# Expert results taken between the last expert blocks, in a four-layer kernel with two mixtures of experts in a row

## The chip, the cores and the metric

The kernel runs on one core of a Trainium2 chip. The metric is the device time of one execution in microseconds (us), smaller being better. Beside the run times there is one profiled execution of each kernel, from which all durations below come.

## The reference

`x` is (4, 512, 256) in float32: four batches of 512 tokens of 256 features. `ctx` is (4, 64, 256). Four layers follow one another, each with an attention onto the context and a feed-forward part, both added to `x`:

```python
# layer 0
x = x + cross_attention(layernorm(x), ctx)             # 16 heads
x = x + experts(layernorm(x), top2 of 8, F=704)        # SwiGLU experts
# layer 1
x = x + feature_map_attention(layernorm(x), ctx)       # exp(z), exp(-z) features
x = x + latent_attention(rmsnorm(x))                   # causal, 16 heads, rotary
x = x + shared_expert(n) + experts(n, top2 of 7, F=256)
# layer 2
s = unit(layernorm(x)) @ unit(ctx).T                   # (512, 64) a batch
x = x + ctx[argmax(s)]                                 # hard alignment
x = x + down(fp4(silu(fp4(n) @ Wg) * (fp4(n) @ Wu)))   # F=704, weights fp4 too
# layer 3
x = x + linear_attention(layernorm(x), ctx)
x = x + experts(layernorm(x), top2 of 8, F=512)
```

`experts` is, for each token, the sum of two expert outputs with the router's weights. `fp4` rounds groups of 16 values to a four-bit grid with a common scale.

## The kernel before

The 2048 tokens are 16 row tiles of 128 (`NT = 16`); a batch `g` is four of them (`GT = 4`). `x` stays on the chip for all four layers.

A mixture of experts is an object of class `Routed`. `route` scatters every token's normed row twice to DRAM (`xs`), in the order of its two experts. The sorted rows make 39 blocks of 128 rows (38 in layer 1), each with one expert. `blocks` loops over them. One pass of the loop over `b` has these parts:

- `up(b)`: transpose the 128 tokens (`ps_xe`, copied to `e_xT`), multiply by the gate and up weights (`ps_gu`), take silu on ACT (`e_s`) and the product on DVE (`e_h`). In its middle it calls `between`, which transposes the block before (`turn`: `ps_he`, `e_hT`) and takes a step of `routing`.
- `down(b-1)`: multiply by the down weights (`ps_de`), scale (`e_y`), and write the rows to `ys` in DRAM by an indirect DMA of POOL, the "put".
- a step of `other`, a generator of work for later; in layer 0 it quantises the weights of layer 2 (`l2_weights`: `w2y`, `ps_wq`, `w2q`).
- `weights(b+3)` and `tokens(b+5)` issue the loads of a later block on SP's queue: 1408 + 768 KB of weights in layer 0, 512 + 256 in layer 1, 1024 + 512 in layer 3, and 130 KB of tokens. `e_wgu` has three buffers, `e_wd` four and `e_x` five.

The rest of `other` is drained after the last `down`.

In the blocks, DVE's and SP's instructions stand in the order of the program text (`in_order`). Those of PE, ACT and POOL are ordered by a scheduler when the kernel is built, from estimated costs; in parts of the attentions PE's order is that of the text as well.

When the blocks are over, `load(t)` reads tile `t`'s two result rows per token from `ys` (256 KB, `e_r`) and `take(t)` adds them to `x[t]` in two adds of 128 x 256. Layer 1's `xattn` does that in `ctx_heads`, batch by batch, ahead of a layer norm (`ln_st`, `ln_mv`, `ln_sd`, `xn`), the transposes (`ps_xT`, `xnT`), the queries (`ps_qf`, `q`) and the first scores (`ps_cs`). Layer 2's `l2` loads its weights (2.1 MB) and prepares the context (`l2_context`: `csq`, `cnr`, `cn`, `ps_cn`), loads and takes all tiles, and then, for each batch, runs `l2_xattn` (norm, `ps_xT`, `sq`, `ps_sim`, the argmax `am_...`, `ps_oh`, `ps_al`), `normed` (a norm into `l2xn`) and, for each tile, `quantized` (`fp4` on DVE and POOL into `xq`, `ps_xq`) ahead of the products `ps_f`. At the end of layer 3 all 16 tiles are loaded, taken and stored to `out_x`, on two queues in turn.

The token order is such that `cuts` splits the blocks by batch: a block below `cuts[g+1]` needs tokens of batches 0 to `g` alone.

Of the kernel before, what the change touches and what calls it, by code (L numbers as in the profile page):

```python
# [22 lines left out]
P = 128  # L23
# [165 lines left out]
class Net:  # L189
# [427 lines left out]

    def ctx_heads(self, pool, st, query, values, bias, before):

        g = st.g  # L620
        if before:
            for i in range(GT):
                before.take(g * GT + i, self.nc.gpsimd if g else self.nc.vector)
        xn = self.xn_tile()
        self.layernorm(g, xn)
        for i in range(GT):
            x = self.x[g * GT + i]
            self.nc.gpsimd.tensor_tensor(x, x, self.row(bias), ALU.add)
        yield
        xT = self.transposed(xn)  # L630
        yield
        st.qs = query(pool, xT)
        yield
        st.va = values(pool, g)
        yield

    def xattn(self, query, values, scale, dv, W, bias, before=None, after=None, keys=None, begin=lambda: None):
# [4 lines left out]
        with self.room("xattn") as pool, self.banks(mm=4, sc=1), ExitStack() as stack:  # L642
# [9 lines left out]
            sts = [SimpleNamespace(g=g, pr=[]) for g in range(B)]  # L652

# [145 lines left out]
class Routed:  # L799
# [9 lines left out]
    def __init__(self, net, n, F, gu, d, name, stamp, w=None):  # L809
# [5 lines left out]
        self.scattered, self.put, self.loaded = [], [], {}  # L815
# [277 lines left out]
    def blocks(self, pool, routing, per=1, other=()):  # L1093
# [4 lines left out]
        other = iter(other)  # L1098
# [4 lines left out]
        def between():  # L1103
            nonlocal turned
            turned = last and self.turn(last[1])
            next(routing, None)

        for b in range(self.nb):
            now = self.up(b, between)
            if last:  # L1110
                self.down(turned, *last)
            last = now
            for _ in range(per - 1):
                next(routing, None)
            next(other, None)
            if b + 5 == self.cuts[-2]:
                for _ in routing:
                    pass
            self.weights(b + 3)
            self.tokens(b + 5)  # L1120
        between()
        self.down(turned, *last)
        for _ in other:
            pass

    def load(self, pool, t, eng, bufs=16):

        net = self.net
        rows = net.ys[self.stamp : self.stamp + 2 * NT * P].rearrange("(k t p) e -> t p k e", p=P, k=2)
        self.loaded[t] = pool.tile([P, 2, E], F32, tag="e_r", name="e_r", bufs=bufs)  # L1130
        eng.dma_start(self.loaded[t], rows[t])

    def take(self, t, eng):

        x, r = self.net.x[t], self.loaded.pop(t)
        for k in range(2):
            eng.tensor_tensor(x, x, r[:, k], ALU.add)


class Layers(Net):  # L1140
# [275 lines left out]
    def l1_ffn(self):  # L1416
        nc, d = self.nc, self.d
        moe = Routed(self, 7, E, d["e1gu"], d["e1d"], "e1", STAMP, w=V_LN2)
        with ExitStack() as stack:

            tail = self.tail = stack.enter_context(self.room("mla_tail"))
            mla, once = (stack.enter_context(ExitStack()) for _ in range(2))
# [18 lines left out]
            def soon():  # L1441
                once.close()
                moe.begin(stack.enter_context(self.room("l1h", side="right")))
# [4 lines left out]
            with self.room("l1b", side="right") as pool, self.banks(mm=4, tr=2, acc=2), self.in_order(DVE, SP):  # L1448
                moe.blocks(pool, last, 3)
        return moe  # L1450

    def l2_context(self, pool):
# [7 lines left out]
        nc.scalar.activation(nr, ss, AF.Sqrt)  # L1460
        nm = pool.tile([SC, B], F32, tag="cnm", name="cnm", bufs=1)
# [3 lines left out]
        cnT = pool.tile([P, NC, B, SC], F32, tag="cnT", name="cnT", bufs=1)  # L1465
        cn = pool.tile([SC, B, E], F32, tag="cn", name="cn", bufs=1)
        nc.vector.tensor_tensor(cn, self.ctx, rs[:, :, None].to_broadcast([SC, B, E]), ALU.mult)
        for c in range(NC):
# [4 lines left out]
        return cnT  # L1473

    def l2_xattn(self, pool, g, cnT):
# [3 lines left out]
        self.layernorm(g, xn)  # L1479
# [3 lines left out]
        nc.scalar.activation(l2, sq, AF.Sqrt)  # L1483
        nc.vector.tensor_scalar(lm, l2, 1e-12, None, ALU.max)
        nc.vector.reciprocal(lr, lm)
        ps = self.acc.tile([P, GT, SC], F32, tag="acc", name="ps_sim")
        for i in range(GT):
            for c in range(NC):
                nc.tensor.matmul(
                    ps[:, i], xT[:, c, i * P : (i + 1) * P], cnT[:, c, g], start=(c == 0), stop=(c == NC - 1)  # L1490
                )
        sim = pool.tile([P, GT, SC], F32, tag="sim", name="sim")
        nc.vector.tensor_tensor(sim, ps, lr[:, :, None].to_broadcast([P, GT, SC]), ALU.mult)
        _, oh = self.first_max(sim, SC, "am")
        pt = self.tr.tile([SC, GT, P], F32, tag="tr", name="ps_oh")
# [3 lines left out]
        nc.scalar.copy(ohT, pt)  # L1499
        for k in range(GT // 2):  # L1500
            pa = self.acc.tile([P, 2, E], F32, tag="acc", name="ps_al")
            for i in range(2):
                nc.tensor.matmul(pa[:, i], ohT[:, 2 * k + i], self.ctx[:, g], start=True, stop=True)
            for i in range(2):
                x = self.x[g * GT + 2 * k + i]
                nc.vector.tensor_tensor(x, pa[:, i], x, ALU.add)
# [92 lines left out]
    def l2(self, moe):  # L1599
        nc = self.nc  # L1600
        F, H = 704, 352
        with self.room("l2") as pool:
            wq = pool.tile([P, W2_END], F32, tag="w2", name="w2", bufs=1)
            whole = W2_END - E
            nc.sync.dma_start(wq[:, :whole], self.w2q[:, :whole])
            nc.sync.dma_start(wq[: F - 5 * P, whole:], self.w2q[: F - 5 * P, whole:])
            wg, wu = (wq[:, a : a + NC * F].rearrange("p (c f) -> p c f", c=NC) for a in (W2_GATE, W2_UP))
            wd = wq[:, W2_DOWN:].rearrange("p (f e) -> p f e", e=E)
            cnT = self.l2_context(pool)
            xns = {}  # L1610

            def tmp(tag, n):
                return pool.tile([P, n], F32, tag=f"{tag}{n}", name=tag)

            def quantized(t):

                g, i = divmod(t, GT)
                xq = pool.tile([P, E], F32, tag="xq", name="xq")
                self.fp4(tmp, xq, xns[g][:, i], nc.gpsimd)
                ps = self.tr.tile([P, NC, P], F32, tag="tr", name="ps_xq")  # L1620
                for c in range(NC):
                    nc.tensor.transpose(ps[:, c], xq[:, c * P : (c + 1) * P], self.ident)
                xT = pool.tile([P, NC, P], F32, tag="xqT", name="xqT")
                nc.scalar.copy(xT, ps)  # L1624
                return xT

            def up(xT):
                pss = []
                for k in range(2):
                    for w in (wg, wu):  # L1630
                        ps = self.mm.tile([P, 512], F32, tag="mm", name="ps_f")
                        for c in range(NC):
                            nc.tensor.matmul(  # L1633
                                ps[:, :H], xT[:, c], w[:, c, k * H : (k + 1) * H], start=(c == 0), stop=(c == NC - 1)
                            )
                        pss.append(ps)
                return pss

            def gated(pss):
                h = pool.tile([P, F], F32, tag="h", name="h")  # L1640
                for k in range(2):
                    s = pool.tile([P, H], F32, tag="fs", name="fs")
                    nc.scalar.activation(s, pss[2 * k][:, :H], AF.Silu)
                    nc.vector.tensor_tensor(h[:, k * H : (k + 1) * H], s, pss[2 * k + 1][:, :H], ALU.mult)
                hq = pool.tile([P, F], F32, tag="hq", name="hq")
                self.fp4(tmp, hq, h, nc.gpsimd)
                return hq

            def down(t, hq):
                hT = pool.tile([P, 6, P], F32, tag="hqT", name="hqT")  # L1650
                self.rows_to_columns(hq, lambda f0, n, r: hT[:r, f0 : f0 + n])
                po = self.acc.tile([P, 512], F32, tag="acc", name="ps_fd")
                for f in range(6):
                    r = min(P, F - f * P)
                    nc.tensor.matmul(po[:, :E], hT[:r, f], wd[:r, f], start=(f == 0), stop=(f == 5))
                nc.vector.tensor_tensor(self.x[t], po[:, :E], self.x[t], ALU.add)

            def normed(g):
                xns[g] = pool.tile([P, GT, E], F32, tag="l2xn", name="l2xn")
                self.layernorm(g, xns[g])  # L1660

            for t in range(NT):
                moe.load(pool, t, nc.scalar if t // GT == 1 else nc.sync)
            for t in range(2 * GT):
                moe.take(t, nc.vector if t < GT else nc.gpsimd)
            self.l2_xattn(pool, 0, cnT)
            normed(0)
            xT, last = quantized(0), None  # L1670
            for t in range(NT):
                g, i = divmod(t, GT)
                if g + 1 < B:
                    if i == 0:
                        if g + 2 < B:
                            for k in range(GT):
                                moe.take((g + 2) * GT + k, nc.gpsimd)
                        self.l2_xattn(pool, g + 1, cnT)
                    elif i == 2:
                        normed(g + 1)  # L1680
                pss = up(xT)
                if t + 1 < NT:
                    xT = quantized(t + 1)
                hq = gated(pss)
                if t:
                    down(t - 1, last)
                last = hq
            down(NT - 1, last)
# [45 lines left out]

# [45 lines left out]
```

## Time and profile before

| what | us |
|---|---|
| runs | 1991.52, 1987.32, 1986.11 (median 1987.32) |
| profiled execution | 1997.21 |
| its span | 1995.5 |
| PE busy in the span | 1712.2 |
| DVE busy in the span | 1020.4 |
| ACT busy, POOL busy | 671.4, 424.3 |
| expert blocks of layer 0 | about 165 to 530 |
| expert blocks of layer 1 | about 1180 to 1344 |
| expert blocks of layer 3 | about 1720 to 1966 |

Times in the profile count from the span's start. "Busy" is the time in which an engine executes an instruction. The granted clock (PEclk) is the share of full speed at which TensorE was let run; its mean over the span is 0.93. A row of the timeline gives start, duration, engine, line and operation, output and inputs, and in brackets the idle time of the engine before it with what ended that. Lines such as SPq and ACTq are DMA issues of the SP and ACT queues. A row of a window gives, for a stretch of time, the busy time of each engine, the granted clock, the busy share of the DMA engines and what they moved.

### The profile page before, as it was taken

How to read it: one execution, taken by the hardware profiler on the slowest of the kernel's cores; microseconds unless marked ns; L12 is line 12 of the kernel's file. 1: busy time of each engine (PE TensorE's matmuls, PEld its weight loads, DVE VectorE, ACT ScalarE, POOL GpSimd, SP SyncE). 2: the span in 40 equal slices, each digit the busy share in tenths (PEclk: the TensorE clock that was granted, in tenths of full speed). 3: DMA queues.
4: the chain of work that ended last, by engine and by line, in shares of the span. 5: the costliest groups of instructions: out<-in, count | busy, mean ns of one | idle time of the engine just before them, and what ended most of it. 6: DMA issues, size and time to landing. Idle time of an engine off the chain costs nothing.

```text
span 1995.5 us, 25928 instructions
## 1 busy us (share of the span) xinstructions
PE 1712.2 (86%) x8752; PEld 970.5 (49%) x8752; DVE 1020.4 (51%) x3011; ACT 671.4 (34%) x1254; POOL 424.3 (21%) x594
## 2 busy tenths in 40 slices
PE   5878999999789868898989888985998887899993
PEld 2435666666444433343433344543665443455552
DVE  3655544444454343444454536546989565553333
ACT  3333222222254323335343432233445334222220
POOL 2031211111240021123131312223113103221112
PEclk8989999999899968998999999995899898999997
DMA  9528787887400100000001035972000001788884
GB/s 294 160 84 330 273 294 281 290 287 281 134 1 1 39 1 1 1 1 22 1 27 42 19 101 173 298 254 85 1 1 1 12 1 65 238 293 301 298 298 162
DMA packets 109350, 271.61 MB, mean 136 GB/s; under 512 B 13409, under 2 KB 71201, under 8 KB 99105
## 3 DMA queue, kind: packets, MB, share of 16 engines
q1 hardware_dynamic: 82976, 227.97, 33.9%
q0 software_dynamic: 10176, 28.00, 3.7%
q10 hardware_dynamic: 16064, 13.98, 2.1%
q8 instruction: 70, 1.15, 0.2%
q14 instruction: 64, 0.52, 0.1%
HBM read 220.48 MB, written 49.42 MB: 135 GB/s over the span
## 4 chain that ended last, share of the span: by engine, by line
PE 69%; DVE 18%; ACT 6%; issue 3%; DMA 2%; POOL 1%; SPq 0%; ACTq 0%; DVEq 0%; POOLq 0%
PE ps_gu L1030 20%; PE ps_de L1072 10%; PE ps_ms L1235 4%; PE ps_mo L1273 3%; DVE mq L1240 2%; PE ps_p L612 2%; PE ps_mx L1250 2%; PE ps_f L1633 2%; PE ps_xT L377 2%; PE ps_he L1059 2%; PE ps_bc L591 2%; ACT cpr L563 2%; PE ps_cx L557 1%; PE ps_ms L1238 1%; PE ps_cy L597 1%
## 5 line engine op out<-in xcount | busy, mean ns | idle before, releaser
L1030 PE MATMUL ps_gu<-e_wgu,e_xT 128*128 128x352 f32 (+1 forms) x1088 | 420.9, 526 | 13.1 <-DVE e_xT L1022 5.8
L1030 PEld LDWEIGHTS ps_gu<-e_wgu,e_xT 128*128 128x128 f32 x1088 | 195.5, 190 | 155.7 <-issue 71.4
L1072 PE MATMUL ps_de<-e_wd,e_hT 128*128 128x256 f32 x932 | 233.0, 387 | 10.8 <-ACT e_hT L303 3.1
L1075 POOL DMA_INDIRECT ys<-e_y,e_to x116 | 113.2, 976 | 482.6 <-ACT e_y L1074 336.5
L1072 PEld LDWEIGHTS ps_de<-e_wd,e_hT 128*128 128x128 f32 x932 | 172.8, 191 | 83.6 <-issue 39.0
L1047 DVE TENSOR_TENSOR e_h<-e_s,ps_gu 128x352 f32<-128x352 f32 (+2 forms) x155 | 83.4, 538 | 244.8 <-PE ps_gu L1030 185.0
L1240 DVE TENSOR_REDUCE mq<-ps_ms 128x2 f32<-128x256 f32 (+3 forms) x128 | 105.7, 826 | 139.9 <-PE ps_ms L1238 136.6
L1046 ACT ACTIVATE e_s<-ps_gu 128x352 f32<-128x352 f32 (+2 forms) x155 | 74.1, 478 | 280.3 <-PE ps_gu L1030 264.9
L1074 ACT ACTIVATE e_y<-ps_de,e_wt 128x256 f32<-128x256 f32 x116 | 55.0, 474 | 262.6 <-PE ps_de L1072 250.0
L1252 ACT ACTIVATE mpr<-ps_mx 128x1024 f32<-128x1024 f32 (+3 forms) x128 | 90.1, 704 | 146.9 <-PE ps_mx L1250 137.9
L1235 PE MATMUL ps_ms<-mkT,mqT 32*128 32x512 f32 (+3 forms) x512 | 111.7, 515 | 25.8 <-DVE mq L1240 24.3
L859 POOL DMA_INDIRECT xs<-xn,e_at x96 | 94.5, 985 | 120.4 <-DVE e_fi L893 39.7
L1250 PE MATMUL ps_mx<-mqm,mkT 32*128 32x128 f32 (+3 forms) x512 | 107.4, 497 | 1.3 <-ACT mpr L1252 1.3
L1254 POOL TENSOR_SCALAR_AFFINE_SELECT mpr<-mpr 128x256 f32<-128x256 f32 x128 | 52.2, 409 | 250.7 <-ACT mpr L1252 250.6
L1273 PE MATMUL ps_mo<-mpr,va 128*32 128x128 f32 (+3 forms) x512 | 97.1, 461 | 4.5 <-POOL mpr L1254 3.2
L1633 PE MATMUL ps_f<-w,xqT 128*128 128x352 f32 x256 | 86.1, 478 | 1.2 <-ACT xqT L1624 1.2
L1059 PE MATMUL ps_he<-consts_sb,e_h 128*128 128x128 f32 x466 | 76.3, 277 | 9.6 <-DVE e_h L1047 6.7
L557 PE MATMUL ps_cx<-q,kbd 32*128 32x512 f32 x256 | 45.2, 806 | 44.1 <-ACT cpr L563 44.1
L1235 PEld LDWEIGHTS ps_ms<-mkT,mqT 32*128 32x128 f32 x512 | 40.9, 195 | 80.6 <-DVE mq L1240 56.0
L1019 DVE COPY e_xT<-ps_xe 128x256 f32<-128x256 f32 x78 | 33.0, 423 | 86.7 <-PE ps_xe L1016 86.7
L377 PE MATMUL ps_xT<-consts_sb,xn 128*128 128x128 f32 x256 | 48.8, 330 | 32.4 <-ACT xn L345 18.7
L1059 PEld LDWEIGHTS ps_he<-consts_sb,e_h 128*128 128x128 f32 x466 | 53.7, 138 | 29.4 <-DVE e_h L1047 13.7
(317 smaller groups left out, 2816.0 us busy)
## 6 DMA issues: line engine op xcount, KB each, us to landing
e_wgu<-in_e0gu SPq DMA_DIRECT2D x39, 1408.0 KB
e_wgu<-in_e3gu SPq DMA_DIRECT2D x39, 1024.0 KB
e_wd<-in_e0d SPq DMA_DIRECT2D x39, 768.0 KB
e_wd<-in_e3d SPq DMA_DIRECT2D x39, 512.0 KB
e_wgu<-in_e1gu SPq DMA_DIRECT2D x38, 512.0 KB
xs<-z SPq DMA_DIRECT2D x16, 1040.0 KB
e_x<-xs SPq DMA_DIRECT2D x116, 130.0 KB
e_wd<-in_e1d SPq DMA_DIRECT2D x38, 256.0 KB
```

The lines of the kernel that those rows point to most:

```text
L377: nc.tensor.transpose(ps[:, i * P : (i + 1) * P], x[:, i, c * P : (c + 1) * P], self.ident)
L859: r = nc.gpsimd.indirect_dma_start(out=net.xs, out_offset=bass.IndirectOffsetOnAxis(ap=at[:, k, i : i + 1], axis=0), in_=rows[:, i], in_of ...
L1030: nc.tensor.matmul(ps[:, :n], xT[:, c], wgu[:, c, cols], start=(c == 0), stop=(c == NC - 1))
L1059: self.nc.tensor.transpose(ps[:r, f - f0], h[:, f * P : f * P + r], net.ident)
L1072: nc.tensor.matmul(po[:, :E], hT[:r, f], wd[:r, f], start=(f == 0), stop=(f == self.nf - 1))
L1075: r = nc.gpsimd.indirect_dma_start(out=net.ys, out_offset=bass.IndirectOffsetOnAxis(ap=at, axis=0), in_=y, in_offset=None)
L1235: nc.tensor.matmul(ps[:, r, :n], st.qT[o][rows, diag], st.kT[o][rows, :n], start=True, stop=False)
L1240: nc.vector.tensor_reduce(st.q[:, i, at : at + 2, HD], ps[:, :, :n], AX.X, ALU.max, negate=True)
L1250: nc.tensor.matmul(ps[:, r, :n], st.kT[o][rows, keys], st.qm[o][rows, j * P :], start=True, stop=True)
L1252: nc.scalar.activation(pr[:, :, :n], ps[:, :, :n], AF.Exp, scale=HD**-0.5)
L1273: nc.tensor.matmul(st.po[32 * n : 32 * n + 32, j * P :], st.va[:, j, at : at + 32], pr[:, r, : S - j * P], start=(j == 0), stop=(j == GT - 1),
L1633: nc.tensor.matmul(ps[:, :H], xT[:, c], w[:, c, k * H : (k + 1) * H], start=(c == 0), stop=(c == NC - 1))
```

## The change

`Routed` gets a list `sure`: for each batch the number of blocks after which its results are complete, [25, 25, 31, 39] with eight experts and [25, 25, 30, 38] with seven. `blocks` gets a generator `ahead`, of which a step is taken in each block from `sure[1] + 2` on (with `rate=2` one more in `between`). `first_results` is such a generator: once batch `g` is complete it loads the four tiles (SP's queue, eight buffers), waits a step, takes two tiles a step on POOL, and calls `then` for each.

- Layer 0: `ahead` takes batches 0 to 2 and does batch 0's norm, bias adds and transposes of layer 1 (`ctx_normed`).
- Layer 1: from block 14 on, `other` closes rooms of the attention, opens layer 2's room, loads its weights (`w2`) and prepares its context. `ahead` takes batches 0 to 2 and steps through `l2_xattn`, `l2_normed` and `quantized` of batch 0.
- Layer 3: `ahead` takes batches 0 to 2 and stores them.
- In all layers `load` passes over tiles that are loaded already, so that only tiles 12 to 15 are left for the end. The rest of `other` is drained ahead of the last `turn` and `down`, not behind them.

```diff
+        self.sure = [self.cuts[-2] + n] * 2 + [(2 * (B - 1) * S + n * (P - 1)) // P, self.nb]
...
-    def blocks(self, pool, routing, per=1, other=()):
+    def blocks(self, pool, routing, per=1, other=(), since=0, ahead=(), rate=1):
...
             next(routing, None)
+            if b >= self.sure[1] + 2 and rate == 2:
+                next(ahead, None)
...
-            next(other, None)
+            if b >= since:
+                next(other, None)
...
             self.weights(b + 3)
             self.tokens(b + 5)
+            self.at = b
+            if b >= self.sure[1] + 2:
+                next(ahead, None)
+        self.at = self.nb
+        for _ in other:
+            pass
         between()
         self.down(turned, *last)
-        for _ in other:
+        for _ in ahead:
             pass
...
+    def first_results(self, pool, then=lambda t: None):
+        for g in range(B - 1):
+            while self.at < self.sure[g] + 2:
+                yield
+            tiles = range(g * GT, (g + 1) * GT)
+            for t in tiles:
+                self.load(pool, t, self.nc.sync, bufs=8)
+            yield
+            for t in tiles[::2]:
+                yield
+                for k in range(2):
+                    self.take(t + k, self.nc.gpsimd)
+            yield
+            for t in tiles:
+                then(t)
...
+    def ctx_normed(self, st, bias, fine=False):
+        xn = self.xn_tile()
+        for _ in self.layernorm_steps(st.g, xn):
+            if fine:
+                yield
+        for i in range(GT):
+            x = self.x[st.g * GT + i]
+            self.nc.gpsimd.tensor_tensor(x, x, self.row(bias), ALU.add)
+        yield
+        st.xT = self.transposed(xn)
+        yield
...
-                moe.blocks(pool, last, 3)
+                rooms = []
+                def later():
+                    tails.close()
+                    rooms.append(stack.enter_context(self.room("l2")))
+                    yield from self.l2_begin(rooms[0])
+                def ahead():
+                    yield from self.l2_ahead(rooms[0], moe)
+                moe.blocks(pool, last, 3, later(), moe.cuts[-2] - 4, ahead(), 2)
...
+    def l2_ahead(self, pool, moe):
+        self.l2xn = {}
+        results = moe.first_results(pool)
+        while GT - 1 not in moe.took:
+            next(results)
+            yield
+        yield
+        yield
+        for steps in (self.l2_xattn(pool, 0), self.l2_normed(pool, 0), self.quantized(pool, 0)):
+            for _ in steps:
+                next(results, None)
+                yield
+        yield from results
...
-                    moe.blocks(pool, self.route(moe, B - 1, self.rw3, fine=True))
+                    moe.blocks(
+                        pool, self.route(moe, B - 1, self.rw3, fine=True), ahead=moe.first_results(pool, store)
+                    )
...
-                    for t in range(NT):
-                        moe.load(pool, t, queues[t % 2])
-                    for t in range(NT):
+                    for t in range((B - 1) * GT, NT):
+                        moe.load(pool, t, queues[t % 2], bufs=8)
+                    for t in range((B - 1) * GT, NT):
                         moe.take(t, nc.gpsimd if t % 3 == 2 else nc.vector)
-                        queues[t % 2].dma_start(out[:, t], self.x[t])
+                        store(t, queues[t % 2])
```

`l2_xattn` is the same work as before, cut into steps by `yield`; the takes of batch 0 in layers 1 and 2 move from DVE to POOL.

## The prediction

> **What bounds the kernel now.** I read the page's slices first, then the windows view over three stretches of expert blocks and over the boundary that follows each, then the timeline inside the boundaries, then the waits of the SP DMA queue.
>
> ```profile
> 430.00:530.00 100.00, 97.83 (x405) 66.19 (x403) 47.13 (x154) 23.27 (x60) 15.14 (x19) 1.00 0.60 214
> 530.00:551.00 21.00, 8.32 (x21) 4.24 (x21) 8.73 (x26) 8.85 (x18) 11.39 (x20) 0.61 0.69 224
> 1300.00:1344.00 44.00, 39.63 (x135) 21.00 (x134) 21.02 (x93) 11.68 (x28) 11.89 (x13) 1.00 0.77 263
> 1345.00:1385.00 40.00, 14.41 (x55) 11.12 (x56) 24.25 (x84) 15.74 (x48) 19.51 (x27) 0.52 0.35 109
> 1860.00:1966.00 106.00, 103.57 (x378) 63.21 (x377) 36.94 (x122) 22.90 (x42) 16.55 (x18) 1.00 0.74 255
> 1967.00:1995.00 28.00, 0.00 (x0) 0.00 (x0) 13.27 (x22) 0.00 (x0) 8.81 (x11) 0.58 0.71 230
> ```
>
> Columns: length, busy time of PE, PEld, DVE, ACT, POOL, granted clock, DMA share, GB/s. In the blocks PE is busy 90 to 98% and DVE, ACT and POOL have half their time free. In the boundaries PE works 8.3 of 21, 14.4 of 40 and 0 of 28 us, at a clock of 0.5 to 0.6. These 89 us are what the change aims at. Why they are empty is in the timeline:
>
> ```profile
> 1966.43 0.47 ACT L1074 ACTIVATE e_y<-ps_de,e_wt 128x256 f32<-128x256 f32 x1 [2.74 <-PE ps_de L1072]
> 1967.18 0.97 POOL L1075 DMA_INDIRECT ys<-e_y,e_to  x1 [2.24 <-ACT e_y L1074]
> 1969.60 8.99 ACTq L1131 DMA_DIRECT2D e_r<-ys  x8
> 1969.71 9.29 SPq L1131 DMA_DIRECT2D e_r<-ys  x8
> 1973.81 13.65 DVE L1137 TENSOR_TENSOR x<-x,e_r 128x256 f32<-128x256 f32 x22 [9.46 <-DMA e_r<-ys]
> 1979.74 8.14 ACTq L1758 DMA_DIRECT2D out_x<-x  x8
> 1980.11 7.06 SPq L1758 DMA_DIRECT2D out_x<-x  x8
> ```
>
> The last put lands, then 16 loads of 256 KB, 32 adds and 16 stores follow in series, though 12 of the 16 tiles were complete 8 blocks earlier. After L0 and L1 it is the same, with a norm and transposes behind it.
>
> **L0 to L1 boundary.**
>
> ```profile
> 538.45 1.68 DVE L1137 TENSOR_TENSOR x<-x,e_r 128x256 f32<-128x256 f32 x4 [0.86 <-DMA e_r<-ys]
> 546.76 3.78 PE L511 MATMUL ps_qf<-xnT,fw_sb 128*128 128x512 f32 x4
> 547.47 1.28 ACT L513 ACT_TABLE_LOAD   x1
> 551.33 1.90 PE L526 MATMUL ps_cs<-kbd,q 32*128 32x128 f32 x56
> ```
>
> Removed from the chain: loads (first add 535.91), 8 adds on DVE, the norm, ps_xT and the half-speed ps_qf; ps_cs starts 21.7 us after the last ps_de (ended 529.6). In the built order all this, even ps_qf and ps_vf, stands ahead of the last ps_de. What is late next: the remaining quantisation of L2's weights is now drained ahead of the last turn, not behind it. Its rows run to about 531 on DVE, so ps_he starts about 532, e_hT is ready at 533, the last ps_de ends at 536. Then table load (1.28), four exponentials (2.7), ps_cs near 539.3. This is 12 us earlier. Against it: 8 ps_xT (1.1 us warm) and ps_qf enter blocks where PE is 98% busy, and two table loads (silu to sqrt and back) sit ahead of an e_s: 2 to 3 us. DVE (24.3 of 50 us) and POOL (8.3 of 50) hold bn_stats (4 x 0.57), adds (8 x 0.72) and bias adds (4 x 0.72) at nothing; without that cover DVE alone would add 2.3. Gain 9 (5 to 12).
>
> **L3 tail.** Removed: 12 loads, 24 adds, 12 stores. Left: the put landed at 1969.6 as now; four loads land by 1974.2 (the first add now waits to 1973.81); eight adds over DVE and POOL, 1.2 us after; four stores of 128 KB from 1975.8, 0.5 MB at about 300 GB/s, last byte near 1978. DMA in the present tail is busy until about 1989 and the span ends 6 us later; so the end is 1983.8. Gain 11.7 (8 to 13). What moves: 1.05 MB at block 27, 1.57 MB (stores too) at 31 and 35 (the last behind all weights) on the SP queue, each in front of weights. At 300 to 346 GB/s that is 3.0 to 5.2 us of delay. Its cover is the prefetch:
>
> ```profile
> SPq L994 <- PE ps_gu L1030: 96.1, 34, 8.1
> SPq L994 <- PE ps_gu L1030: 43.9, 30, 3.9
> ```
>
> First line L3, second L1 (waits of the SP queue: total, times, longest). The queue stops until ps_gu frees a weight buffer, 2.8 us a block in L3: weights are fetched two blocks (12 us) ahead of use and need about 7, so 5 to 8 us are free. No PE wait on e_wgu is listed there, so I cost the L3 and L0 transfers at nothing; without the cover it would be 8 us in L3. The puts now wait for loads ahead of them on POOL (the loads land 2.8 us after issue), within a period of 6.2 us; e_y has six buffers, so ACT and PE don't wait for it.
>
> **L1 to L2 boundary.** This is the hard part: here the whole chain is put into L1 blocks of 3.5 to 3.95 us.
>
> ```profile
> 1360.49 3.68 PE L1489 MATMUL ps_sim<-cnT,xnT 128*128 128x64 f32 x16 [0.57 <-DVE xnT L305]
> 1365.12 0.90 DVE L715 TENSOR_TENSOR am_eq<-sim,am_m 128x256 f32<-128x256 f32 x1
> 1369.64 2.92 PE L1503 MATMUL ps_al<-ctx_sb,ohT 64*128 64x256 f32 x6 [0.67 <-ACT ohT L1499]
> ```
>
> From the end of ps_gu of block 30 (1314.5) to ps_sim of batch 1 (1389.2), 74.7 us now. After: blocks 31 to 37 as now (27), their stretch, and about 8 for the last turn, down and batch 1's remaining norm. The stretch: DVE gains about 21 us of ops in its hand-written order (norms 5, argmax 2.6, x adds 1.7, quantisation of tile 0 and of tiles 1 to 3 11) where it has 23 of 44 us free, at least 13 of them in front of an op that PE waits for; ACT's five table pairs, 8 xn and 8 sq (20 us, spread over 7 blocks) put at most 5.9 ahead of a single e_s. I take 24 (13 to 28), so 59, a gain of 15.7. Against it:
> - Clock. The trace has a case of work inserted in an L1 block:
>
> ```profile
> 1208.45 1.98 PE L1030 MATMUL ps_gu<-e_wgu,e_xT 128*128 128x512 f32 x4 [0.70 <-DVE e_xT L1022]
> 1212.70 0.33 PE L1059 MATMUL ps_he<-consts_sb,e_h 128*128 128x128 f32 x1 [2.27 <-DVE e_h L1047]
> 1216.22 3.78 PE L1030 MATMUL ps_gu<-e_wgu,e_xT 128*128 128x512 f32 x4 [1.83 <-DVE e_xT L1022]
> ```
>
> The second ps_gu takes 3.78 for 1.98 after idles of only 2.27 and 1.83 us. The Trainium skill ("TensorE: Matmul & The Clock Gate", "HAM oscillation") halves the clock only after a gap of over some 3.4 us. By the rule the stretched blocks stay warm and cost 0; by the row about every other one pays 1.9 on ps_gu. I take the row for two of them: 4.
> - L2's context (sum of squares, sqrt, scaling, 8 transposes) and w2 (2.1 MB) enter blocks 14 to 17. ACT 1.6 + 1.28 + 0.2 + 1.28 before an e_s, of which 2.6 is not covered; DVE's cn 1.22, PE's ps_cn 1.08; w2 takes 6.2 us of DMA, against a longest free 3.9. Sum 5.5 (3 to 9).
> - From there on the built order of PE interleaves ps_xe and ps_de as it now does from block 26; periods are 3.51 before that and 3.95 after. Nine blocks x 0.44 = 4.
> - The three loads of 1.05 MB, in blocks 27, 30 and 32, wait on SP for the last put (2.4 us from its start to the load's issue in the trace) with the next weights behind them, and take 3.1 us of DMA. The put starts about 1.5 us behind ps_gu, so weights due 3.5 us after ps_gu start 0.4 late and run beside the load: 3.5 us late of 3.9 free. I take 0; at worst 3 each.
>
> Net 15.7 - 13.5 = 2 (-10 to 15). The rule that speaks most against the change is "ScalarE: Activation LUTs" ("What ACT_TABLE_LOAD costs"): 1283 ns for a switch and 1380 ns of drain. The trace has 1283 and the next ACTIVATE 0.02 us later (load 1346.51, cnr 1347.81). The change adds 12 loads in L1 blocks; by the row 15.4 us of ACT, in the sums above; by the rule 16.6 more, of which half would stand ahead of an e_s: 8 less gain, 15 in all rather than 23. I take the row.
>
> **Sum.** 9 + 11.7 + 2 = 23. The profiled execution took 1997.2 (span 1995.5 and 1.7 around it), 0.5% over the median of the runs, 1987.3. So 1974 for such an execution, 1965 against the median.
>
> **Rivals.**
> - Transfers not hidden (slower). Seven result loads, one group of stores and w2, 9.9 MB in all (7 x 1.05, 0.5, 2.1), stand ahead of weights on the one queue, whose blocks already run at a DMA share of 0.77 to 0.89. At 345 GB/s they are 29 us, and the loads' waits for puts 7 x 2.4 = 17 more: 23 - 46 gives 2010 if nothing hides. It decides where a load's delay passes the prefetch slack, 3.9 us in L1, 5 to 8 elsewhere. For it: L1's 3.5 of 3.9 is close. Against it: today the queue waits for PE, not PE for the queue. Chance 0.11.
> - L1's pieces cost what the routing did (no change). Around the rows above ps_gu to ps_gu is 9.6 us for 3.95; seven blocks x 5.65 = 40 for 24: 16 less gain, plus up to 6 for context: about 1987. For it: the same mix of DVE and ACT pieces. Against it: routing is a longer serial chain per block. Chance 0.15.
> - L1 at its DVE minimum and warm (faster still): stretch 13 and no clock loss: 15 more, 1950. Chance 0.20.
> - The scheduler undoes it (the moved steps run late all the same, for lack of banks or buffers): 1980 or so. The built order shows them in the blocks, so 0.05.
> - The forecast: 0.49.
>
> **Numbers.** A measurement of this kernel tells about 0.3% (6 us) from no change. Forecast and the faster rival lie wholly beyond it, the scheduler rival too, the second is half same, a quarter each side; of the first nearly all is slower. Faster 0.79, same 0.09, slower 0.12. The range takes in the L1 bounds: 1946 to 1987; the dearest cases are left out.
>
> **What would show it.** Right: ps_cs within 4 us of the last ps_de of L0; DVE's e_r rows gone from both first boundaries; from the last put to the span's end about 16.5 us for 28; L0 and L3 block periods unchanged at 9.3 and 6.2. L1: blocks 31 to 37 at about 7 us each, PE's clock under 1 in one or two of them, blocks 15 to 17 longer by 5 in sum. Wrong: PE waits on DMA e_wgu in the blocks (first rival), ps_gu of 3.8 us in most blocks past 30 (second), L1's periods unchanged (third), ps_cs over 10 us behind ps_de (fourth).

## The result, and the profile after

The changed kernel takes 1972.0 us (median of four runs, 1971.8 to 1972.6) where the kernel before, in runs beside it, took 1986.7: a ratio of 0.9926, 95% interval 0.9903 to 0.9949. A second timing, of six runs against eleven on another chip, gave 0.9919 (0.9904 to 0.9934), 16 us. Forecast were 22 us and a range of 1946 to 1987, with faster as the likeliest; the range reaches up to the time of before. The medians of before differ by up to 9 us between the chips used (1986.7 to 1996.1), so below ratios are compared, each with runs of the kernel before on its own chip.

The first profile of before took 1997.2 us and that of after 1971.8, a difference of 25. Ten of these are not the change's: a second profile of before (e1 below) took 1985.8, and reaches the first product of layer 1's experts 10 us sooner. It is the base of this table.

| mark, us from the span's start | before (e1) | after | earlier by |
|---|---|---|---|
| last `ps_gu` of layer 0 ends | 523.8 | 526.3 | -2.5 |
| last `ps_de` of layer 0 ends | 530.9 | 542.0 | -11.1 |
| first `ps_cs` of layer 1 | 551.6 | 544.6 | 7.0 |
| last `ps_cs` of layer 1 | 659.5 | 654.2 | 5.3 |
| first `ps_ms` (scores of the latent attention) | 733.9 | 726.4 | 7.5 |
| first `ps_gu` of layer 1 | 1159.1 | 1156.7 | 2.4 |
| last `ps_gu` of layer 1 ends | 1332.9 | 1368.3 | -35.4 |
| first `ps_f` of layer 2 | 1377.7 | 1371.3 | 6.4 |
| last `ps_de` of layer 3 ends | 1955.5 | 1950.4 | 5.1 |
| end of the span | 1984.1 | 1970.1 | 14.0 |

The three boundaries moved, but what they gained was partly paid inside the blocks. The fall from 7.5 to 2.4 us across the latent attention can't be put down to the change: from the first `ps_ms` to the first `ps_gu` the two profiles of before need 437.0 and 425.2 us, and after needs 430.3. The windows view of after, over the stretches that answer to those of before (length, busy time of PE, PEld, DVE, ACT and POOL, granted clock, DMA share, GB/s):

```profile
430.00:530.00 100.00, 97.47 (x406) 65.90 (x405) 52.83 (x159) 27.94 (x66) 33.72 (x46) 1.00 0.69 249
530.00:551.00 21.00, 12.60 (x95) 8.98 (x93) 7.80 (x19) 7.12 (x16) 6.11 (x12) 0.75 0.26 80
1312.90:1374.40 61.50, 43.79 (x142) 24.81 (x141) 35.63 (x139) 33.64 (x68) 27.77 (x36) 0.81 0.45 152
1951.00:1970.00 19.00, 0.00 (x0) 0.00 (x0) 3.02 (x6) 0.00 (x0) 2.49 (x3) 0.57 0.30 97
```

Layer 0's blocks took in the new work with PE still 97% busy and POOL's time doubled (33.7 for 15.1). The boundary behind layer 1 is gone as an empty stretch, but its last seven blocks and what follows now run at a clock of 0.81 with PE busy 71% of the time.

**Layer 0 to 1.** The timeline around the last product of layer 0:

```profile
535.03 0.51 POOL L1613 TENSOR_TENSOR w2y<-w2y,f_sc 128x192 f32<-128x192 f32 x1 [2.33 <-DVE w2y L1612]
535.76 0.60 PE L1073 MATMUL ps_he<-consts_sb,e_h 128*128 128x128 f32 x4
537.41 4.59 PE L1086 MATMUL ps_de<-e_wd,e_hT 128*128 128x256 f32 x12
542.53 1.28 ACT L513 ACT_TABLE_LOAD   x1
544.57 1.75 PE L526 MATMUL ps_cs<-kbd,q 32*128 32x128 f32 x20 [2.56 <-ACT q L513]
...
551.46 3.80 PE L526 MATMUL ps_cs<-kbd,q 32*128 32x128 f32 x64 [2.64 <-DVE mx L534]
```

The drained quantisation (`w2y`) holds `ps_he` until 535.8. PE, idle in between, then runs the last 12 `ps_de` in 4.59 us (2.95 a block earlier). The first scores (`ps_cs`) come in two halves of 64 products, which take 4.25 and 3.80 us at a granted clock of 0.50 (546.3 to 555.3). In the first profile of before they took 2.12 and 2.07, but that one is the exception: e1 has 2.67 and 3.70, and e3 and e4, whose layer 0 is that of before, have 2.88 and 3.80, 2.57 and 3.50. The row of e1:

```profile
556.96 3.70 PE L526 MATMUL ps_cs<-kbd,q 32*128 32x128 f32 x64 [2.64 <-DVE mx L534]
```

So the half-clock stretch lay over `ps_xT` and `ps_qf` (3.78 in before) and a part of the scores; it now lies over all of these scores. It was not removed; against e1, e3 and e4 it costs the scores 1 to 2 us more.

**Layer 1 to 2.** The first adds of results meet the norm in block 31:

```profile
1316.68 0.99 POOL L1089 DMA_INDIRECT ys<-e_y,e_to  x1 [0.17 <-issue]
1317.70 0.73 POOL L1167 TENSOR_TENSOR x<-x,e_r 128x256 f32<-128x256 f32 x1
1318.46 0.43 DVE L336 BATCH_NORM_STATS2 ln_st<-x 128x6 f32<-128x256 f32 x1 [3.03 <-POOL x L1167]
1319.03 0.58 DVE L1036 TENSOR_SCALAR e_xT<-ps_xe,vecs_sb 128x128 f32<-128x128 f32 x2
1319.40 3.78 PE L1044 MATMUL ps_gu<-e_wgu,e_xT 128*128 128x512 f32 x4 [5.08 <-DVE e_xT L1036]
```

POOL's last add of batch 0 stands between puts; the norm's statistics wait for it on DVE, whose order is fixed, and behind them `e_xT`, for which PE waits: 5.08 us idle and a `ps_gu` of 3.78 for 1.88. The chain of waits between 1302 and 1319 runs through a put, the loads, POOL's adds and this norm, not through PE.

**Layer 3's end.** The same lines as before the change, now for four tiles:

```profile
1951.17 0.99 POOL L1089 DMA_INDIRECT ys<-e_y,e_to  x1 [0.69 <-ACT e_y L1088]
1953.61 0.89 SPq L1158 DMA_DIRECT2D e_r<-ys  x2
1957.36 1.68 DVE L1167 TENSOR_TENSOR x<-x,e_r 128x256 f32<-128x256 f32 x4 [9.02 <-DMA e_r<-ys]
1958.27 2.61 SPq L1860 DMA_DIRECT2D out_x<-x  x2
1958.92 1.58 POOL L1167 TENSOR_TENSOR x<-x,e_r 128x256 f32<-128x256 f32 x2 [6.76 <-DMA e_r<-ys]
1959.07 2.10 ACTq L1860 DMA_DIRECT2D out_x<-x  x2
1959.33 1.45 DVE L1167 TENSOR_TENSOR x<-x,e_r 128x256 f32<-128x256 f32 x2 [0.29 <-DMA e_r<-ys]
```

From the last put to the end it is 18.9 us for 27.8 in e1: 2.4 from the put to the loads, 3.7 until the first add, 3.4 for the adds. What ends the span behind them is not the stores, whose last packet is through at 1962.3. It is a `DRAIN` of POOL, an instruction at the end of the program that starts with POOL's last add and takes 9.58 us. The source view of the program's end, in after and then in before (count; shortest, median and longest in ns; first and last start in us):

```profile
L1890 POOLq DRAIN  x3: 45/107/9580, 1959.7 to 1969.8; - x3
L1776 POOLq DRAIN  x3: 45/107/9577, 1985.1 to 1995.2; - x3
```

In all 14 profiles of this record the span ends 9.57 us after the end of POOL's last add (1960.50 in after, 1985.93 in before). So layer 3's part, in the profile, is the time by which POOL's last add comes sooner: 9.3 us after the last put, for 18.2 in e1. No run takes the last adds from POOL, so whether its `DRAIN`, and with it the end, would then come sooner is not shown.

### The profile page after: what moved, and what is told of

Same layout as the page of the kernel before. It is cut to its first block, busy times and chain, and to the rows that moved or that the text cites. A ratio compares the mean times of both kernels' runs of the same rounds, so it can differ in the third digit from the quotient of the medians.

```text
span 1970.1 us, 25945 instructions
## 1 busy us (share of the span) xinstructions
PE 1713.7 (87%) x8752; PEld 972.3 (49%) x8752; DVE 1007.7 (51%) x2979; ACT 684.3 (35%) x1265; POOL 448.9 (23%) x626
## 4 chain that ended last, share of the span: by engine, by line
PE 68%; DVE 17%; ACT 7%; issue 3%; POOL 2%; DMA 2%; ACTq 0%; SPq 0%; DVEq 0%; POOLq 0%
PE ps_gu L1044 20%; PE ps_de L1086 9%; PE ps_ms L1283 4%; PE ps_mo L1321 3%; PE ps_p L612 2%; DVE mq L1288 2%; PE ps_f L1731 2%; PE ps_mx L1298 2%; PE ps_bc L591 2%; PE ps_he L1073 2%; PE ps_xT L377 2%; ACT cpr L563 2%; PE ps_cx L557 1%; PE ps_cy L597 1%; ACT xn L345 1%
## 5 line engine op out<-in xcount | busy, mean ns | idle before, releaser
L1044 PE MATMUL ps_gu<-e_wgu,e_xT 128*128 128x352 f32 (+1 forms) x1088 | 429.3, 535 | 21.7 <-DVE e_xT L1036 14.6
L1086 PE MATMUL ps_de<-e_wd,e_hT 128*128 128x256 f32 x932 | 239.0, 394 | 10.8 <-ACT e_hT L303 4.8
L1167 POOL TENSOR_TENSOR x<-x,e_r 128x256 f32<-128x256 f32 x90 | 66.7, 751 | 84.5 <-DMA e_r<-ys 81.0
```

What stands on the lines that cost most here:

```text
L1044: nc.tensor.matmul(ps[:, :n], xT[:, c], wgu[:, c, cols], start=(c == 0), stop=(c == NC - 1))
```

## The experiments

Theory after the result: the three parts add, layer 1's being near nothing because its blocks grow by as much as its boundary shrinks. The rival: they don't add, since what one part gains a later stage gives back. The next four separate the parts.

### e1: the kernel before, once more

> The kernel before, unchanged, for a second profile of it. Its profiled execution shown so far (1997.2 us) lies 10 us over its median; if that is the kernel's own spread, this one lies nearer 1987 and the lost time is in the attention stages that the change leaves alone (layer 1's latent attention), not in the expert blocks or boundaries. If the two profiles agree to 3 us everywhere, the difference of the two traces is the change's own and the medians are off.

It took 1985.8. Up to the first `ps_ms` the two profiles of before are 1.4 us apart (732.5 and 733.9); from there to the first `ps_gu` of layer 1 they need the 437.0 and 425.2 us named above. Nearly all of the difference of these two profiles lies in that attention, which the change leaves alone.

### e2, e3, e4: one layer's part alone

e2 keeps the changes of layer 0 (with the drain), e3 those of layer 1, e4 those of layer 3; the rest is as before. The edit of e4, for the pattern:

```diff
                         moe.blocks(
-                            pool, self.route(moe, B - 1, self.rw0, fine=True), other=later(), ahead=ahead()
+                            pool, self.route(moe, B - 1, self.rw0, fine=True), other=later()
                         )
...
-                moe.blocks(pool, last, 3, later(), moe.cuts[-2] - 4, ahead(), 2)
+                moe.blocks(pool, last, 3)
```

> Layer 0's part alone (results of three batches, batch 0's norm, transposes, and the earlier draining of the weight quantisation); layers 1 and 3 as before. The prediction's size for this part, 9 us, gives 1978. The trace of the changed kernel shows 3.3 us left when layer 1's first probabilities are multiplied: 1983.

> Layer 1's part alone; layers 0 and 3 as before. Prediction: gain 2, so 1985. Reading of the two traces: blocks 0 to 30 lose 11.3, block 30 to the alignment of batch 1 gains 13.2, layer 2 another 1 to 2: 1983 to 1985. If preparing inside the blocks cost what routing did (the rival of no change), it is 1987 or above.

> Layer 3's part alone; layers 0 and 1 as before. Prediction: 11.7 us, so 1975. From the trace of the changed kernel (last product to the end 19.7 for 29.1): 9.4 us, so 1977. If the transfers were not hidden, the blocks would be longer and it would be over 1980.

| kernel | ratio | 95% interval | us of 1988 |
|---|---|---|---|
| e2, layer 0 alone | 0.9963 | 0.9948 to 0.9978 | -7.4 |
| e3, layer 1 alone | 1.0002 | 0.9991 to 1.0014 | +0.4 |
| e4, layer 3 alone | 0.9942 | 0.9927 to 0.9958 | -11.5 |

Their sum is -18.5; the whole gave -15 and -16, within the intervals of the three. So the parts add, as far as this can be told, and layer 1's brings nothing that these runs can tell from zero, though it is the largest edit. In its trace the first `ps_f` comes 5.5 us earlier than e1's, yet the end only 2.5 us (1981.6 for 1984.1). That can't be read as a loss behind layer 1, for from `ps_f` to the end the two profiles of before differ by 4.6 us themselves (611.0 and 606.4; e3 has 609.4). e3's eleven runs average no gain at all.

### e5 and e6: the drained quantisation, put into the blocks instead

e5 takes a second step of `other` in each of layer 0's last ten blocks, so that nothing is left to drain. e6 adds to that the preparation of layer 2's context, moved from layer 1's blocks to layer 0's, in pieces of one batch that fit layer 0's buffers.

```diff
             if b >= since:
                 next(other, None)
+            if b >= self.nb - 10:
+                next(other, None)
...
     # e6, layer 0's later():
             yield from self.ctx_ready(kept, self.keys_features)
+            yield from self.l2_context(pool)
             yield from self.l2_weights(pool)
```

> The changed kernel, but layer 0's last ten blocks take two steps of the weight quantisation each, so that nothing of it is left to drain ahead of the last turn. Theory: the drain holds up the last product (ended 542.0, for about 531 without it) and leaves PE idle, so that the first scores start at half clock; both go: scores start near 534 for 544.6, 7 to 10 us less in all, 1962 to 1965. Rival: something behind (the maxima, the loads of the last batch) sets the pace of layer 1's attention and the gain is lost again there: 1970 or more.

> As e5, and layer 2's context is prepared in layer 0's blocks instead of layer 1's blocks 15 to 17. Theory: those two blocks (7.3 and 5.0 us) return to 3.5, and PE's order stays the plain one up to block 26, 5.3 + 3 = 8 us less than e5 less 1 to 2 for layer 0: 1956 to 1958. Rival: the weights of layer 2 (2.1 MB), which still load there, make the delay: no more than 2 us less than e5.

Both expectations failed. e5 gave 0.9931 (0.9913 to 0.9948), no better than the change, and e6 0.9985 (0.9975 to 0.9996). In e5 the last `ps_gu` of layer 0 ends at 534.7 for 526.3 while the last `ps_de` ends at 541.9 as before: the blocks grew by what the drain had taken. In e6 they grew to 550.4. The timeline of e5, in a block where the adds of results meet the quantisation:

```profile
463.50 0.29 DVE L1611 TENSOR_SCALAR w2y<-w2y 128x256 int32<-128x256 int32 x1
464.15 0.43 DVE L1613 TENSOR_TENSOR w2y<-w2y 128x256 f32<-128x256 f32 x1
...
473.82 6.12 POOL L1169 TENSOR_TENSOR x<-x,e_r 128x256 f32<-128x256 f32 x8 [7.10 <-DMA e_r<-ys]
474.79 0.67 DVE L1611 TENSOR_SCALAR w2y<-w2y 128x192 int32<-128x192 int32 x1
476.19 0.87 DVE L1613 TENSOR_TENSOR w2y<-w2y 128x192 f32<-128x192 f32 x1
478.84 5.51 PE L1044 MATMUL ps_gu<-e_wgu,e_xT 128*128 128x352 f32 x12 [2.25 <-DVE e_xT L1033]
```

While POOL adds, DVE's steps take twice as long on tiles that are smaller (0.67 for 0.29, 0.87 for 0.43); `e_xT` is late, PE idles 2.25 us and 12 `ps_gu` run in 5.51 for 3.82. In e6 there is a second hold beside it: `ps_wq` stands in PE's order ahead of the next block's `ps_xe`, and the POOL product it needs stands behind the eight adds.

```profile
476.45 6.33 POOL L1169 TENSOR_TENSOR x<-x,e_r 128x256 f32<-128x256 f32 x8 [7.38 <-DMA e_r<-ys]
482.74 0.62 POOL L1618 TENSOR_TENSOR w2y<-w2y,f_sc 128x256 f32<-128x256 f32 x1
483.41 0.48 PE L1644 MATMUL ps_wq<-consts_sb,w2y 128*128 128x128 f32 x1 [4.86 <-POOL w2y L1618]
```

PE is idle 4.86 us there, and 13.5 us in nine such waits between 440 and 555. So DVE's and POOL's half-empty time in the blocks is no free cover for work on both.

### e7: layer 1's results alone in its blocks

The alignment, norm and quantisation of batch 0 go behind the blocks again; loads, adds and context stay inside.

```diff
     def ahead():
-        yield from self.l2_ahead(rooms[0], moe)
+        yield from moe.first_results(rooms[0])
...
     def l2(self, pool, moe):
+        self.l2xn = {}
+        for steps in (self.l2_xattn(pool, 0), self.l2_normed(pool, 0), self.quantized(pool, 0)):
+            whole(steps)
```

> The changed kernel, but layer 1's blocks take the results of batches 0 to 2 alone; the alignment, norm and quantisation of batch 0 come behind the blocks, as before the change. If putting them into the blocks pays, blocks 30 to 37 take some 30 us for 54.5 and the stretch from there to batch 1's alignment some 40 for 7, so 4 to 8 us slower than the changed kernel: 1976 to 1980. If it costs what it brings (as the layer's net of zero suggests): 1970 to 1974.

The ratio is 0.9925 (0.9911 to 0.9939), that of the change. Putting batch 0's preparation into the blocks costs what it brings, to within the 4 us that these intervals leave, as the second case of the expectation has it. The windows view of e7, over its last blocks and over the boundary:

```profile
1310.00:1351.00 41.00, 30.42 (x105) 16.53 (x103) 21.94 (x76) 18.02 (x39) 26.43 (x35) 0.96 0.70 240
1351.00:1378.00 27.00, 13.32 (x59) 10.65 (x60) 18.61 (x68) 11.04 (x26) 8.45 (x12) 0.62 0.15 44
```

The blocks keep a clock of 0.96 there, and the slow clock (0.62) sits in the boundary, over fewer matmuls. From the start of block 30 to the first `ps_f` it is 63.6 us for 60.2 in the changed kernel; the times can't tell these 3.4 us.

### e8: batch 0 of layer 1 taken on DVE

```diff
-                    self.take(t + k, self.nc.gpsimd)
+                    self.take(t + k, self.nc.gpsimd if g or not first else first)   # first = DVE
...
-        yield
-        yield
         for steps in (self.l2_xattn(pool, 0), ...
```

> The changed kernel, but in layer 1 batch 0's results are taken on DVE, and two empty steps less follow. Theory: in block 31 DVE's in-order queue waits 3.0 us for POOL's last add, which stands behind three puts, and PE idles 5.1 and falls to half clock: 8 adds on DVE (3.4 us) end before, 3 to 5 us less, 1967 to 1969. Rival: the adds wait for their loads on DVE's queue instead, no gain: 1971 to 1974.

The ratio is 0.9899 (0.9883 to 0.9915), the best of all, but its interval meets those of the change (0.9904 to 0.9934). The theory's mechanism did not hold; the rival's did:

```profile
1306.52 1.68 DVE L1167 TENSOR_TENSOR x<-x,e_r 128x256 f32<-128x256 f32 x4 [4.63 <-DMA e_r<-ys]
1308.12 0.60 DVE L1036 TENSOR_SCALAR e_xT<-ps_xe,vecs_sb 128x128 f32<-128x128 f32 x2
1308.52 3.55 PE L1044 MATMUL ps_gu<-e_wgu,e_xT 128*128 128x512 f32 x4 [6.13 <-DVE e_xT L1036]
```

DVE now waits 4.63 us for the loads with `e_xT` behind it, and PE idles 6.13 for 5.08. From the first `ps_gu` of layer 1 to the first `ps_f` it is 213.8 us for 214.6. If e8 gains time at all, it does not come from that wait.

### e9: the drain behind the last product again

```diff
-        for _ in other:
-            pass
         between()
         self.down(turned, *last)
+        for _ in other:
+            pass
```

> The changed kernel with one edit undone: the rest of layer 0's weight quantisation is drained behind the last turn and down again. Theory: the last product waits on the drain (it ended 542.0, and half of that at half clock); it ends near 531 again, the scores start near 537 instead of 544.6, 5 to 8 us less: 1964 to 1967. Rival: PE's order still has the drain's transposes ahead of the scores, so the scores start as late as now, and nothing changes: 1971 to 1973.

0.9914 (0.9895 to 0.9933): nothing changes, as the rival has it. The last `ps_de` ends at 536.8 for 542.0, but the scores start at 545.2 for 544.6, because ACT's order has the drain's copies ahead of the queries' table load:

```profile
536.82 0.47 ACT L1088 ACTIVATE e_y<-ps_de,e_wt 128x256 f32<-128x256 f32 x1 [3.06 <-PE ps_de L1086]
541.24 0.33 PE L1639 MATMUL ps_wq<-consts_sb,w2y 128*128 128x128 f32 x1 [2.01 <-POOL w2y L1613]
542.33 0.26 ACT L1640 COPY wqT<-ps_wq 64x128 f32<-64x128 f32 x1 [0.45 <-PE ps_wq L1639]
543.13 1.28 ACT L513 ACT_TABLE_LOAD   x1 [0.55 <-ACT wqT L1640]
545.17 4.24 PE L526 MATMUL ps_cs<-kbd,q 32*128 32x128 f32 x63 [2.94 <-ACT q L513]
```

Where the drain is put, the scores wait for it: in e5 by longer blocks, in the change through `ps_he`, here through ACT's queue, with starts at 544.5, 544.6 and 545.2. In e9's profile layer 0's first two blocks take 17.9 us for 15.1, for a reason that stays open; counted from the last `ps_gu`, the scores start after 15.7 us for 18.3. So some 2.6 us may have been won here and lost at the start. Here too the scores run at half clock (4.24).

### e10: layer 2's context early in layer 0

The context takes the place of the two empty steps at the start of layer 0's `later`.

```diff
     def later():
-        yield
-        yield
+        yield from self.l2_context(pool)
         W3.extend(self.load_xattn("w_qT", "w_kvT", "w_oT"))
```

> The changed kernel, but layer 2's context is prepared in layer 0's first two blocks (in place of two empty steps), not in layer 1's blocks 15 to 17. e6 had it at layer 0's end together with doubled quantisation steps, and those blocks grew by 24 us. Theory: e6 lost by quantisation steps that meet POOL's adds; early there are none, and layer 1's blocks 16 and 17 fall from 7.3 and 5.0 us to 3.5, its plain PE order lasts to block 26: 6 to 8 us less, 1964 to 1966. Rival: the loads of layer 2's weights cause the long blocks: 1970 to 1973.

0.9952 (0.9938 to 0.9966), slower than the change by 0.3%. In layer 1 the two long blocks fell only to 5.96 and 4.39 us from 7.29 and 5.02, and PE's order is interleaved from there on all the same. That is 2 us less for the two, but e3 and e5, which have the context there as the change has it, took 10.6 as well, for 10.4 here and 12.3 in the change; in the change the second block's `ps_gu` ran cold (3.08 for 1.88). What lengthens these blocks stays open: in e10 PE waits for no weights there, so the rival is not shown either. The loss is in layer 0's first two blocks, which took 8.5 and 11.1 us for 6.2 and 8.9: PE waits 2.3 us there for the context's scaled rows, and the last `ps_de` of layer 0 ends 3.6 us later (545.6). That is less than the 0.3% (6 us), and e11, which has the same edit and the same first two blocks, is not slower than the change; the rest is not explained.

### e11: e8, e9 and e10 together

> The changed kernel with e8's (batch 0 of layer 1 taken on DVE), e9's and e10's edits together. If they add up: 1972 less 3.6, less 6, less 7: 1955. If layer 1's attention gives back what comes early in layer 0, 1962; if none of the three holds, 1968.

0.9906 (0.9890 to 0.9922), the last of the expected cases: not told apart from the change, nor from e8 alone.

### e12: the change once more

> The changed kernel itself, timed against the kernel before in five rounds, as the base for e5 to e11. If the three parts add up (ratios 0.9963, 1.0002, 0.9942), the ratio is 0.9907 or 18 us; the first timing, against four runs of before, gave 0.9926 or 15 us. Against e7 and e9 (0.9925, 0.9914) no difference is expected; if it lies at 0.9926 or above, e8's 0.9899 is a gain, and at 0.9907 it is none that can be told.

0.9919 (0.9904 to 0.9934), between the two cases. On this base none of e5, e7, e8, e9 and e11 can be told from the change; e6 and e10 lie above its interval.

## Why the prediction was right

**The order of the parts and the sign.** Faster, with layer 3's end as the largest part, layer 0 second and layer 1 near zero: forecast 11.7, 9 and 2, measured alone 11.5, 7.4 and -0.4. Against the forecast's 22.7 the whole gave 15 to 16, about two thirds of it. The intervals of the parts are 2 to 3 us wide on either side, so that the runs hardly tell which term fell short; what follows on the terms is read from the profiles.

**Layer 3.** The blocks kept their pace (242.6 us from the first `ps_gu` to the end of the last, for 243.6 in e1), with 2.1 MB of results and 0.5 MB of stores ahead of weights: the cover that the prediction named, the queue's waits for PE, held. The waits of the SP queue in after, layer 3 and then layer 1:

```profile
SPq L1008 <- PE ps_gu L1044: 86.5, 31, 9.5
SPq L1158 <- DMA ys<-e_y,e_to: 14.1, 3, 6.3
...
SPq L1008 <- PE ps_gu L1044: 55.4, 25, 5.5
SPq L1158 <- DMA ys<-e_y,e_to: 42.0, 4, 29.8
```

The columns are total, times and longest; the 29.8 is the wait of the last batch's loads for the last put. The queue still stops for PE, and no wait of PE on weights is listed in either stretch, nor in layer 0 from 430 to 530. This is what speaks against the rival of unhidden transfers. Put to end it is 18.9 us for the 16.6 that was forecast. The adds took 3.4 us and not 1.2, since six of the eight stand on DVE and the loads land one by one; but the first stores move while the last adds still run, and the last byte moved 11.1 us after the put, for 10.8 by the forecast (1978). The term that was mis-sized lies behind it. The forecast took over the 6 us of before, from the end of the transfers to the end of the span, and it is 7.8, because the end hangs on POOL's last add and its `DRAIN` and not on the stores. By the profile the part is 8.9 us, by the runs 11.5 (8.3 to 14.5).

**Layer 0.** The scores start 7.0 us earlier, where 12 less 2 to 3 was forecast. The blocks' stretch was right (2.5). The end of the drain was misread: 531 was taken for DVE's last piece, but it ended at 532.7 even in before, and at 534.9 in after, with the last `ps_de` at half clock on top (1.6). So the last `ps_de` ended at 542.0, not 536. Not foreseen was that PE comes cold to the scores: from the first of them to the end of the second half it is 10.7 us, for 6.8 and 9.0 in the two profiles of before. But this is not lost for good: from the first score to the first `ps_ms` it is 181.9 us for 181.2 and 182.2, so the 7 us stay, and e2's 7.4 agrees.

**Layer 1.** Here the sum came out, and in part by luck. From the first `ps_gu` to the end of block 30, where 9.5 us of loss were forecast (context 5.5, order of PE 4), it is 156.3 us for 146.9: 9.4. From block 30 to batch 1's `ps_sim` it is 61.5 for 72.9 in e1, 11.4 of gain; forecast were 15.7 less 4 for the clock. (The 1389.2 that the prediction gives for this `ps_sim` is where it ends, not where it starts.) The seven blocks grew by 27.7 us where 24 + 4 had been taken, but the slow clock cost 6.7 on `ps_gu` alone and not 4, so that the rest took 21 and not 24: two errors that nearly cancel. Net 2.0 for 2, the small difference of two large terms. It depends on the profile chosen: from the first `ps_gu` to this `ps_sim` the four profiles with layer 1 as before (before, e1, e2, e4) need 216.2 to 219.8 us, and after, e3 and e12 215.3 to 218.1. The times (e3) show no gain.

**The clock.** The prediction took the trace's row over the rule of the Trainium skill ("TensorE: Matmul & The Clock Gate", "HAM oscillation"), which asks for no idle gaps of PE over some 3.4 us. In blocks 31 to 37 `ps_gu` took 3.78, 1.94, 2.97, 1.98, 2.89, 3.62 and 2.77 us, 6.7 over seven warm ones. The first followed 5.08 us of idle time, as the rule would have it; the third and fifth followed 2.94 and 2.12, and ahead of the last two no gap is over 2.2. Read for single gaps the rule would give 1.9 of the 6.7. The row was right to take, but the clock fell in five of the seven blocks, where the prediction had one or two.

**The table loads.** The rule that spoke most against the change ("ScalarE: Activation LUTs", "What ACT_TABLE_LOAD costs": 1.38 us of drain with each load) is not borne out, and the row was right to take. ACT's rows around a load in block 32:

```profile
1323.88 0.18 ACT L354 ACTIVATION_READ_ACCUMULATOR sq<-xn 128x1 f32 x1
1324.08 1.28 ACT L1060 ACT_TABLE_LOAD   x1
1325.37 0.38 ACT L1060 ACTIVATE e_s<-ps_gu 128x256 f32<-128x256 f32 x1
```

ACT is idle for 0.02 us ahead of it and 0.01 behind. All 102 loads of after take 1.28 us, and around 75 of them ACT is idle for less than 1.0 us in all, before and behind together.

**The rivals.** The rival that priced layer 1's pieces like the routing rows had 67 us for its seven blocks, the forecast 51 to 55. They took 8.3, 8.3, 7.3, 7.7, 5.9, 10.3 and 6.7 us, 54.5 in sum, so the forecast's price held. The faster rival, warm blocks at DVE's minimum, had nothing of it. The rival of steps that run late had the scores over 10 us behind the last `ps_de`; it is 2.6.

## What to carry to other kernels

Half-empty engines in a stretch were cover only for work that meets nobody in their queues: ask of each piece which instruction stands behind it on an engine whose order is fixed, and who waits for that one. A boundary's serial chain was worth taking apart where nothing has to be computed from it (layer 3's loads and stores, 11.5 us for a few lines), and not where every link must be computed by the same engines in blocks of a few microseconds (layer 1, zero for most of the diff). The slow clock stayed with the gap: with work moved across it, the next matmuls ran slow (the scores at layer 0's boundary). Look at what ends the span itself: here it is POOL's last add, not the last store. And take a second profile of the kernel before: here its spread is as large as most of the differences that were to be explained.

## What the runs showed of the hardware

- POOL's adds slow DVE. Steps on 128 x 192 tiles in SBUF took 0.67 (`TENSOR_SCALAR`) and 0.87 us (`TENSOR_TENSOR`) on DVE during POOL's adds (e5), for 0.26 and 0.36 outside them (after, at 533.5 and 534.1). A copy out of `ps_xe` was not slowed (0.41 at 478.38, for 0.39 at 467.09). The Trainium skill ("SBUF — State Buffer", "Who interferes with whom") says that a DVE instruction with two SBUF inputs contends with a GpSimd instruction that reads SBUF, and that `tensor_scalar` can contend in a mode that uses both ports, where the one that comes second is blocked for the whole instruction of the other. The contention is there for both; DVE's steps last about two and a half times as long, and the rows don't show whether they stand still for a part of that. The prediction cost POOL's adds beside DVE at nothing.
- POOL's `DRAIN` at the end of the program takes 9.58 us, and the span ends 0.8 us behind it, in all 14 profiles.
- The time of one kernel differs more between the chips used (medians of before 1986.7 to 1996.1) than by most of the edits tried here.
